# One PSUM ring for products and transposes, and W loaded over 128 partitions, in a pairwise bilinear kernel

## The chip, the cores and the metric

The kernel runs on one core of a Trainium2 chip. The metric is the device time of one execution in microseconds (us). Before the change it was 1623.27 us, the median of three runs (1620.51 to 1627.43).

Engines are named as the profile names them: PE is TensorE's matmul side, PEld its weight loads, DVE is VectorE, ACT is ScalarE, POOL is GpSimd, SP is SyncE, which here only issues DMAs. PEclk is the share of full speed that TensorE's clock was granted.

## What is computed

The input x has 4096 rows of F = 32 fields with D = 64 numbers each, W one 64x64 matrix for each of the 496 pairs (i, j) with i < j. All is float32. For each row b and each pair, the output is the product of field i with the pair's matrix, times field j element by element:

```python
vi = inputs[:, i_idx, :]
vj = inputs[:, j_idx, :]
vdotw = jnp.einsum('bpd,pde->bpe', vi, W)
inter = vdotw * vj
return inter.reshape(B, -1)
```

The output has 4096 x 31744 numbers, 520 MB, against 33.6 MB of x and 8.1 MB of W.

## The kernel before

**Tiles.** A tile is 128 rows of x; there are 32 of them, fully unrolled. The pairs of one field i are neighbours in the output, so for each i one product of [128, 64] with [64, (31 - i) * 64] gives a run of output columns, and its factors x_j are a run of columns of x itself. W is kept in SBUF for the whole run, in 16 tensors w0 to w15, one for each pair p of neighbouring fields (2p, 2p + 1): the even field's matrices on partitions 0 to 63, the odd one's on 64 to 127. The transposed x, xT, is laid out alike. So the matmuls of the two fields use two halves of the array's rows and run side by side.

**Products (L98 to L117).** A field pair's columns are cut into stretches of 1024. For each stretch and each of the two fields there is one PSUM tile `pm` of two banks (1024 float32). Matmuls cover one bank (512 columns) each, in the order first bank of the even field, first bank of the odd field, second bank of the even field, second bank of the odd field. TensorE takes its instructions in this order. A float32 matmul stands in the trace as two MATMULs, each with a weight load. The widths shrink with i: fields 0 to 15 have a first stretch of 1024 columns (the odd field 15 just so), and a narrower second one; fields 16 to 30 have a single stretch of 960 down to 64 columns. That makes 46 products a tile.

**Multiplication (L121).** VectorE multiplies each `pm` with its run of x and writes into an output buffer `o` in SBUF. This frees the `pm` slot.

**Stores (L124).** The outputs of a tile leave in ten stores, as the list STORES groups the field pairs: pairs 0 to 7 each by themselves, 8 and 9 together, 10 to 15 together. There are five output buffers. The stores are issued on SP, in order, behind the loads of W (L80), which stand on the same queue. Before each issue SP waits for what the DMA needs, and, from the ninth DMA of the program on, for an earlier DMA that used the same one of eight completion counters.

**Transposes (L63 to L70).** TensorE also transposes x: 16 blocks of 128x128 a tile, into PSUM tiles `pt` of one bank (four blocks each), which ScalarE copies to xT. The next tile's x is transposed ahead of store group 5 (PREFETCH_AT). The framework's scheduler places the four groups of one tile's transposes among the products of earlier ones.

**PSUM.** PSUM has eight banks. Three slots of two banks are for `pm`, two slots of one bank for `pt`:

```python
ps_t = ctx.enter_context(tc.tile_pool(name="ps_t", bufs=2, space=bass.MemoryType.PSUM))
ps_m = ctx.enter_context(tc.tile_pool(name="ps_m", bufs=3, space=bass.MemoryType.PSUM))
```

Slots are given out in turn: the first matmul into a slot waits until its last reader has ended.

**Loads.** x tiles come on ScalarE's queue, three buffers, two tiles ahead. W comes on SP as 31 loads over 64 partitions each (field 31 has no pairs).

Of the kernel before, what the change touches and what calls it, by code (L numbers as in the profile page):

```python
# [1 line left out]

# [6 lines left out]

F32 = mybir.dt.float32  # L10
ALU = mybir.AluOpType

P = 128  # batch rows per tile
NPS = 1024  # columns per PSUM tile (two banks)
BANK = 512  # columns per matmul
# Field pairs (i = 2p, 2p + 1) whose outputs leave in one store.
STORES = [[0], [1], [2], [3], [4], [5], [6], [7], [8, 9], [10, 11, 12, 13, 14, 15]]
PREFETCH_AT = 5  # store group before which the next tile's x is transposed


@with_exitstack
def pair_bilinear_kernel(
    ctx: ExitStack,
    tc: tile.TileContext,
    x: bass.AP,  # [B, F * D]
    w: bass.AP,  # [D, NP * D]: w[d, p * D + e] = W[p, d, e]
    out: bass.AP,  # [B, NP * D]
    F: int,
    D: int,
):  # L30
    """out[b, p, e] = x[b, j, e] * sum_d x[b, i, d] W[p, d, e] for each pair p = (i, j), i < j.

    The pairs of one i are neighbours in p, with j = i+1 .. F-1. So for each i one
    product [128, D] x [D, (F-1-i) * D] gives a run of output columns, and its
    factors x_j are the run of columns (i+1) * D .. F * D of x itself.
    Even i live on partitions 0-63 and odd i on 64-127, for W and for the
    transposed x, so that the matmuls of two i share the array's rows.
    """
    nc = tc.nc
    B = x.shape[0]  # L40
    NT = B // P
    NPR = F // 2

    width = [(F - 1 - i) * D for i in range(F)]
    off = [sum(width[:i]) for i in range(F)]
    store_w = [sum(width[2 * p] + width[2 * p + 1] for p in g) for g in STORES]

    const = ctx.enter_context(tc.tile_pool(name="const", bufs=1))
    xpool = ctx.enter_context(tc.tile_pool(name="x", bufs=3))
    xtpool = ctx.enter_context(tc.tile_pool(name="xT", bufs=2))  # L50
    opool = ctx.enter_context(tc.tile_pool(name="o", bufs=5))
    ps_t = ctx.enter_context(tc.tile_pool(name="ps_t", bufs=2, space=bass.MemoryType.PSUM))
    ps_m = ctx.enter_context(tc.tile_pool(name="ps_m", bufs=3, space=bass.MemoryType.PSUM))

    ident = const.tile([P, P], F32, tag="ident", name="ident")
    make_identity(nc, ident)

    def load_x(t):
        xt = xpool.tile([P, F * D], F32, tag="x", name=f"x_{t}")
        nc.scalar.dma_start(out=xt, in_=x[ts(t, P), :])  # L60
        return xt

    def transpose_x(t, xt):  # L63
        xT = xtpool.tile([P, NPR, P], F32, tag="xT", name=f"xT_{t}")
        for g in range(NPR // 4):
            pt = ps_t.tile([P, 4, P], F32, tag="pt", name=f"pt_{t}_{g}")
            for c in range(4):
                nc.tensor.transpose(pt[:, c, :], xt[:, ts(4 * g + c, P)], ident)  # L68
            nc.scalar.copy(xT[:, 4 * g : 4 * g + 4, :], pt)  # L69
        return xT  # L70

    xs = {0: load_x(0)}

    w_sb = []
    for p in range(NPR):
        wp = const.tile([P, width[2 * p]], F32, tag=f"w{p}", name=f"w{p}")
        for h in range(2):
            i = 2 * p + h
            if width[i]:
                nc.sync.dma_start(  # L80
                    out=wp[h * D : (h + 1) * D, : width[i]],
                    in_=w[:, off[i] : off[i] + width[i]],
                )
        w_sb.append(wp)

    xs[1] = load_x(1)
    xTs = {0: transpose_x(0, xs[0])}

    for t in range(NT):
        xt, xT = xs.pop(t), xTs.pop(t)  # L90
        if t + 2 < NT:
            xs[t + 2] = load_x(t + 2)
        for s, group in enumerate(STORES):
            if s == PREFETCH_AT and t + 1 < NT:
                xTs[t + 1] = transpose_x(t + 1, xs[t + 1])
            o0 = off[2 * group[0]]
            osb = opool.tile([P, max(store_w)], F32, tag="o", name=f"o_{t}_{s}")
            for p in group:  # L98
                for c0 in range(0, width[2 * p], NPS):
                    live = []  # L100
                    for h in range(2):
                        i = 2 * p + h
                        n = min(NPS, width[i] - c0)
                        if n > 0:
                            pm = ps_m.tile([P, NPS], F32, tag="pm", name=f"pm_{t}_{i}_{c0}")
                            live.append((h, i, n, pm))
                    for b0 in range(0, NPS, BANK):
                        for h, i, n, pm in live:
                            b1 = min(b0 + BANK, n)
                            if b1 > b0:  # L110
                                nc.tensor.matmul(  # L111
                                    pm[:, b0:b1],
                                    xT[h * D : (h + 1) * D, p, :],
                                    w_sb[p][h * D : (h + 1) * D, c0 + b0 : c0 + b1],
                                    start=True,
                                    stop=True,
                                )  # L117
                    for h, i, n, pm in live:
                        o = off[i] - o0 + c0
                        xj = (i + 1) * D + c0  # L120
                        nc.vector.tensor_tensor(  # L121
                            osb[:, o : o + n], pm[:, :n], xt[:, xj : xj + n], ALU.mult
                        )
            nc.sync.dma_start(  # L124
                out=out[ts(t, P), o0 : o0 + store_w[s]], in_=osb[:, : store_w[s]]
            )


# [18 lines left out]
```

## Time and profile before

| what | us |
|---|---|
| median of three runs | 1623.27 |
| the three runs | 1623.27, 1620.51, 1627.43 |
| span of the profiled execution | 1624.4 |
| PE busy (union) | 1400.6 (86%) |
| DVE busy | 1205.8 (74%) |
| ACT busy | 70.2 (4%) |
| mean DMA share, 104.6 to 1600 us | 0.84, 349 GB/s |

The profiled execution has no time of its own beside its span. The span lies within the runs shown, 1.1 us above their median. PE's busy time is a union of pipelined matmuls and does not mean that the array is full for 86% of the span. The mean granted clock over the run was 0.963.

The chain that ended last, followed back from the last instruction, spends 60% of the span in the products' matmuls (L111), 31% in VectorE's multiplications (L121), 4% in transposes (L68) and 3% in the loads of W. The rows on which the prediction rests are shown there.

### The profile page before, as it was taken

How to read it: one execution, taken by the hardware profiler on the slowest of the kernel's cores; microseconds unless marked ns; L12 is line 12 of the kernel's file. 1: busy time of each engine (PE TensorE's matmuls, PEld its weight loads, DVE VectorE, ACT ScalarE, POOL GpSimd, SP SyncE). 2: the span in 40 equal slices, each digit the busy share in tenths (PEclk: the TensorE clock that was granted, in tenths of full speed). 3: DMA queues.
4: the chain of work that ended last, by engine and by line, in shares of the span. 5: the costliest groups of instructions: out<-in, count | busy, mean ns of one | idle time of the engine just before them, and what ended most of it. 6: DMA issues, size and time to landing. Idle time of an engine off the chain costs nothing.

```text
span 1624.4 us, 13543 instructions
## 1 busy us (share of the span) xinstructions
PE 1400.6 (86%) x5376; PEld 680.8 (42%) x5376; DVE 1205.8 (74%) x1472; ACT 70.2 (4%) x129; POOL 0.7 (0%) x6
## 2 busy tenths in 40 slices
PE   7688888889888888888888888888888898888886
PEld 3344444444444444444444443444444444434443
DVE  4477777777867778777787777787777777777875
ACT  1000000000000000000000000000000000000000
POOL 0000000000000000000000000000000000000000
PEclk9899999999989999999999999999999989999998
DMA  9998888788877888788888878987888878888876
GB/s 243 382 383 370 357 345 348 330 371 355 348 317 321 377 361 346 319 344 347 367 362 342 346 329 376 379 362 320 343 347 373 372 318 334 342 374 367 349 298 289
DMA packets 53231, 562.66 MB, mean 346 GB/s; under 512 B 6192, under 2 KB 6576, under 8 KB 8112
## 3 DMA queue, kind: packets, MB, share of 16 engines
q1 hardware_dynamic: 48560, 528.24, 78.8%
q10 hardware_dynamic: 4608, 33.56, 5.3%
q8 instruction: 42, 0.69, 0.2%
q14 instruction: 21, 0.17, 0.0%
HBM read 41.68 MB, written 520.09 MB: 346 GB/s over the span
## 4 chain that ended last, share of the span: by engine, by line
PE 63%; DVE 31%; DMA 3%; issue 2%; SPq 0%; DVEq 0%
PE pm L111 60%; DVE o L121 31%; PE pt L68 4%; DMA w<-in_w_dram 3%; DMA out_dram<-o 0%; SPq L80 0%; DVEq L121 0%; SPq L124 0%
## 5 line engine op out<-in xcount | busy, mean ns | idle before, releaser
L111 PE MATMUL pm<-w,xT 64*128 64x512 f32 (+7 forms) x4864 | 1333.1, 567 | 210.2 <-DVE o L121 193.3
L121 DVE TENSOR_TENSOR o<-pm,x 128x1024 f32<-128x1024 f32 (+15 forms) x1472 | 1205.8, 870 | 411.3 <-PE pm L111 385.2
L111 PEld LDWEIGHTS pm<-w,xT 64*128 64x128 f32 x4864 | 623.8, 192 | 893.7 <-DVE o L121 637.3
L69 ACT COPY xT<-pt 128x512 f32<-128x512 f32 x128 | 68.9, 589 | 1467.1 <-PE pm L111 759.2
L68 PE MATMUL pt<-ident,x 128*128 128x128 f32 x512 | 78.1, 287 | 6.0 <-DMA x<-in_x_dram 6.0
L68 PEld LDWEIGHTS pt<-ident,x 128*128 128x128 f32 x512 | 56.9, 143 | 42.2 <-issue 41.3
L69 ACT ACT_TABLE_LOAD x1 | 1.3, 1283 | 2.1 <-issue 2.1
masks.py:199 POOL TENSOR_SCALAR_AFFINE_SELECT ident<-ident 128x128 f32<-128x128 f32 x1 | 0.3, 293 | 0.1
masks.py:197 POOL MEMSET ident<- 128x128 f32 x1 | 0.2, 206 | 0.3 <-POOLq L139 0.3
L139 POOL MEMSET const-bfloat16-1.0<- 128x1 bf16 x1 | 0.1, 102 | 0.0
L139 POOL MEMSET const-uint8-127<- 128x1 uint8 x1 | 0.1, 102 | 0.0
L139 POOL MEMSET const-float32-0.0<- 128x1 f32 x1 | 0.1, 99 | 0.2 <-issue 0.2
L139 POOL MEMSET const-float32-1.0<- 128x1 f32 x1 | 0.1, 98 | 0.0
## 6 DMA issues: line engine op xcount, KB each, us to landing
out_dram<-o SPq DMA_DIRECT2D x32, 2112.0 KB, 9.4
out_dram<-o SPq DMA_DIRECT2D x32, 1952.0 KB, 7.9
out_dram<-o SPq DMA_DIRECT2D x32, 1824.0 KB, 7.8
out_dram<-o SPq DMA_DIRECT2D x32, 1728.0 KB, 5.5
out_dram<-o SPq DMA_DIRECT2D x32, 1696.0 KB, 7.5
out_dram<-o SPq DMA_DIRECT2D x32, 1568.0 KB, 7.8
out_dram<-o SPq DMA_DIRECT2D x32, 1440.0 KB, 7.3
out_dram<-o SPq DMA_DIRECT2D x32, 1312.0 KB, 5.7
```

Of the source, the lines that this page charges most:

```text
L68: nc.tensor.transpose(pt[:, c, :], xt[:, ts(4 * g + c, P)], ident)
L69: nc.scalar.copy(xT[:, 4 * g : 4 * g + 4, :], pt)
L111: nc.tensor.matmul(pm[:, b0:b1], xT[h * D : (h + 1) * D, p, :], w_sb[p][h * D : (h + 1) * D, c0 + b0 : c0 + b1], start=True, stop=True,)
L121: nc.vector.tensor_tensor(osb[:, o : o + n], pm[:, :n], xt[:, xj : xj + n], ALU.mult)
L139: nc = bacc.Bacc("TRN2", target_bir_lowering=False, num_devices=1)
```

## The change

All eight banks form one pool of four slots of two banks. Products and transposes take their slots from it in the order in which they stand in the program. A transpose tile is now two banks wide: eight blocks and one ScalarE copy of 1024 columns, twice a tile instead of four times with half the width. The first half of the next tile's x is transposed ahead of store group 5, the second ahead of group 6, each in its own place.

W is laid out by the host as [128, 16384]: for each field pair the even field's matrices on the first 64 rows, the odd field's on the last 64, padded by 64 columns of zeros where the odd field has one matrix less. So each w tensor is one load over all 128 partitions, 16 in place of 31.

```diff
-    ps_t = ctx.enter_context(tc.tile_pool(name="ps_t", bufs=2, space=bass.MemoryType.PSUM))
-    ps_m = ctx.enter_context(tc.tile_pool(name="ps_m", bufs=3, space=bass.MemoryType.PSUM))
+    psum = ctx.enter_context(tc.tile_pool(name="ps", bufs=4, space=bass.MemoryType.PSUM))
...
-    def transpose_x(t, xt):
-        xT = xtpool.tile([P, NPR, P], F32, tag="xT", name=f"xT_{t}")
-        for g in range(NPR // 4):
-            pt = ps_t.tile([P, 4, P], F32, tag="pt", name=f"pt_{t}_{g}")
-            for c in range(4):
-                nc.tensor.transpose(pt[:, c, :], xt[:, ts(4 * g + c, P)], ident)
-            nc.scalar.copy(xT[:, 4 * g : 4 * g + 4, :], pt)
-        return xT
+    def transpose_x(xT, t, xt, g):
+        n = NPS // P
+        pt = psum.tile([P, NPS], F32, tag="ps", name=f"pt_{t}_{g}")
+        for c in range(n):
+            nc.tensor.transpose(pt[:, ts(c, P)], xt[:, ts(n * g + c, P)], ident)
+        nc.scalar.copy(xT[:, ts(g, NPS)], pt)
+
+    def new_xT(t):
+        return xtpool.tile([P, NPR * P], F32, tag="xT", name=f"xT_{t}")
...
-        for h in range(2):
-            i = 2 * p + h
-            if width[i]:
-                nc.sync.dma_start(
-                    out=wp[h * D : (h + 1) * D, : width[i]],
-                    in_=w[:, off[i] : off[i] + width[i]],
-                )
+        nc.sync.dma_start(out=wp, in_=w[:, woff[p] : woff[p] + width[2 * p]])
...
-            if s == PREFETCH_AT and t + 1 < NT:
-                xTs[t + 1] = transpose_x(t + 1, xs[t + 1])
+            if t + 1 < NT and s in (PREFETCH_AT, PREFETCH_AT + 1):
+                if s == PREFETCH_AT:
+                    xTs[t + 1] = new_xT(t + 1)
+                transpose_x(xTs[t + 1], t + 1, xs[t + 1], s - PREFETCH_AT)
...
-                            pm = ps_m.tile([P, NPS], F32, tag="pm", name=f"pm_{t}_{i}_{c0}")
+                            pm = psum.tile([P, NPS], F32, tag="ps", name=f"pm_{t}_{i}_{c0}")
```

On TensorE, around the transposes in the second tile. A name `pm_i_c` is the product of field i from column c on, `pt_g` a group of transposes, the last number of each name a running one; "waits" names the engine or DMA counter whose progress is waited for. Before, from the end of field pair 4 to pair 5's second stretch and the next transposes:

```order
L111 MATMUL pm_9_1024_452<-w_92,xT_243 128x384 [waits DVE_49]
L68 MATMUL pt_2_471<-ident,x_154 128x128 [waits Activation_49]
L68 MATMUL pt_2_471<-ident,x_154 128x128 x3
L68 MATMUL pt_3_477<-ident,x_154 128x128 [waits Activation_49]
L68 MATMUL pt_3_477<-ident,x_154 128x128 x3
L111 MATMUL pm_10_0_484<-w_95,xT_243 128x512 [waits DVE_49]
L111 MATMUL pm_11_0_485<-w_95,xT_243 128x512 [waits DVE_49]
L111 MATMUL pm_10_0_484<-w_95,xT_243 128x512
L111 MATMUL pm_11_0_485<-w_95,xT_243 128x512
L111 MATMUL pm_10_1024_492<-w_95,xT_243 128x320 [waits DVE_49]
L111 MATMUL pm_11_1024_493<-w_95,xT_243 128x256 [waits DVE_49]
L68 MATMUL pt_0_674<-ident,x_369 128x128 [waits DMAHW2_49,Activation_49]
```

The same place in the changed kernel:

```order
L115 MATMUL pm_9_1024_426<-w_85,xT_221 128x384 [waits DVE_49]
L72 MATMUL pt_0_433<-ident,x_132 128x128 [waits DVE_49]
L72 MATMUL pt_0_433<-ident,x_132 128x128 x7
L115 MATMUL pm_10_0_444<-w_87,xT_221 128x512 [waits DVE_49]
L115 MATMUL pm_11_0_445<-w_87,xT_221 128x512 [waits DVE_49]
L115 MATMUL pm_10_0_444<-w_87,xT_221 128x512
L115 MATMUL pm_11_0_445<-w_87,xT_221 128x512
L115 MATMUL pm_10_1024_452<-w_87,xT_221 128x320 [waits DVE_49]
L115 MATMUL pm_11_1024_453<-w_87,xT_221 128x256 [waits Activation_49]
L72 MATMUL pt_1_459<-ident,x_132 128x128 [waits DVE_49]
L72 MATMUL pt_1_459<-ident,x_132 128x128 x7
L115 MATMUL pm_12_0_470<-w_89,xT_221 128x512 [waits DVE_49]
```

The transposes now wait for VectorE (the slot's last reader) instead of ScalarE, and four tiles later in the ring a product, field 11's second part, waits for ScalarE's copy instead of VectorE.

On SP, from the last loads of W to the first stores. Before:

```order
L80 DMA w_122<-in_w_dram 64x192 [waits DMAHW7_49]
L80 DMA w_122<-in_w_dram 64x128 [waits DMAHW0_49]
L80 DMA w_125<-in_w_dram 64x64 [waits DMAHW1_49]
L124 DMA out_dram<-o_0_156 128x3904 [waits DMAHW2_49,DVE_49]
L124 DMA out_dram<-o_1_174 128x3648 [waits DMAHW3_49,DVE_49]
```

After:

```order
L83 DMA w_103<-in_w_dram 128x320 [waits DMAHW0_49]
L83 DMA w_105<-in_w_dram 128x192 [waits DMAHW1_49]
L83 DMA w_107<-in_w_dram 128x64 [waits DMAHW2_49]
L128 DMA out_dram<-o_0_134 128x3904 [waits DMAHW3_49,DVE_49]
L128 DMA out_dram<-o_1_152 128x3648 [waits DMAHW4_49,DVE_49]
```

The order on the queue is the same, with 16 loads instead of 31 ahead of the first store, each over 128 partitions and still each waiting for the DMA eight places earlier.

More of the change, by code (lines that the diff above doesn't have):

```diff
@@ L45, in pair_bilinear_kernel @@
     off = [sum(width[:i]) for i in range(F)]
+    woff = [sum(width[0 : 2 * p : 2]) for p in range(NPR)]
     store_w = [sum(width[2 * p] + width[2 * p + 1] for p in g) for g in STORES]
@@ L76, in pair_bilinear_kernel @@
         wp = const.tile([P, width[2 * p]], F32, tag=f"w{p}", name=f"w{p}")
-        for h in range(2):
-            i = 2 * p + h
-            if width[i]:
-                nc.sync.dma_start(
-                    out=wp[h * D : (h + 1) * D, : width[i]],
-                    in_=w[:, off[i] : off[i] + width[i]],
-                )
+        nc.sync.dma_start(out=wp, in_=w[:, woff[p] : woff[p] + width[2 * p]])
         w_sb.append(wp)
     xs[1] = load_x(1)
-    xTs = {0: transpose_x(0, xs[0])}
+    xTs = {0: new_xT(0)}
+    for g in range(2):
+        transpose_x(xTs[0], 0, xs[0], g)
     for t in range(NT):
@@ L112, in pair_bilinear_kernel @@
                                     pm[:, b0:b1],
-                                    xT[h * D : (h + 1) * D, p, :],
+                                    xT[h * D : (h + 1) * D, ts(p, P)],
                                     w_sb[p][h * D : (h + 1) * D, c0 + b0 : c0 + b1],
@@ L136 @@
     x = np.ascontiguousarray(r_inputs).reshape(B, F * D)
-    w = np.ascontiguousarray(np.transpose(L0_rec_W, (1, 0, 2))).reshape(D, NP * D)
+    wt = np.transpose(L0_rec_W, (1, 0, 2))
+    n = [F - 1 - i for i in range(F)]
+    first = [sum(n[:i]) for i in range(F)]
+    halves = [
+        np.concatenate(
+            [
+                np.pad(wt[:, first[i] : first[i] + n[i]], ((0, 0), (0, h), (0, 0)))
+                for i in range(h, F, 2)
+            ],
+            axis=1,
+        )
+        for h in range(2)
+    ]
+    w = np.ascontiguousarray(np.stack(halves)).reshape(2 * D, -1)
     nc = bacc.Bacc("TRN2", target_bir_lowering=False, num_devices=1)
```

## The prediction

> **What bounds the kernel now.** I read the waits first, then VectorE's timeline over one tile, then the chain, then the DMA share by stretches. The waits (who waited for whom: us in total, times, longest):
>
> ```profile
> DVE o L121 <- PE pm L111: 385.2, 384, 16.3
> PE pm L111 <- DVE o L121: 193.3, 347, 10.1
> DVE o L121 <- DMA out_dram<-o: 13.7, 1, 13.7
> SPq L80 <- DMA w<-in_w_dram: 25.0, 20, 3.9
> ```
>
> TensorE and VectorE wait for each other, VectorE for a store once. The stretches (us; busy time of PE, PEld, DVE, ACT, POOL; PEclk, DMA share, GB/s), the second being one whole tile:
>
> ```profile
> 10.20:47.20 37.00, 30.50 (x112) 13.30 (x112) 19.79 (x20) 2.73 (x5) 0.00 (x0) 1.00 0.99 237
> 178.93:227.32 48.39, 42.12 (x170) 20.28 (x168) 37.69 (x47) 2.15 (x4) 0.00 (x0) 1.00 0.86 358
> 57.00:107.00 50.00, 43.73 (x167) 21.82 (x163) 37.24 (x45) 2.15 (x4) 0.00 (x0) 0.95 1.00 419
> 980.00:1000.00 20.00, 17.41 (x70) 7.60 (x68) 16.41 (x18) 1.07 (x2) 0.00 (x0) 1.00 1.02 432
> ```
>
> At full clock a tile takes 48.39 us. VectorE works 37.69 of them, and the DMA share of 0.86 leaves room. Nobody is full: two engines pass three PSUM slots to and fro. VectorE's timeline of that tile (start, length, count, then the idle time before):
>
> ```profile
> 178.93 4.61 DVE L121 TENSOR_TENSOR o<-pm,x 128x1024 f32<-128x1024 f32 x4 [1.61 <-PE pm L111]
> 183.78 4.34 DVE L121 TENSOR_TENSOR o<-pm,x 128x1024 f32<-128x1024 f32 x4 [0.23 <-PE pm L111]
> 188.49 4.08 DVE L121 TENSOR_TENSOR o<-pm,x 128x1024 f32<-128x1024 f32 x4 [0.37 <-PE pm L111]
> 193.06 3.79 DVE L121 TENSOR_TENSOR o<-pm,x 128x1024 f32<-128x1024 f32 x4 [0.50 <-PE pm L111]
> 197.49 3.35 DVE L121 TENSOR_TENSOR o<-pm,x 128x1024 f32<-128x1024 f32 x4 [0.63 <-PE pm L111]
> 202.65 3.08 DVE L121 TENSOR_TENSOR o<-pm,x 128x1024 f32<-128x1024 f32 x4 [1.81 <-PE pm L111]
> 207.49 2.82 DVE L121 TENSOR_TENSOR o<-pm,x 128x1024 f32<-128x1024 f32 x4 [1.75 <-PE pm L111]
> 211.91 2.49 DVE L121 TENSOR_TENSOR o<-pm,x 128x1024 f32<-128x1024 f32 x3 [1.61 <-PE pm L111]
> 215.10 2.15 DVE L121 TENSOR_TENSOR o<-pm,x 128x960 f32<-128x960 f32 x2 [0.70 <-PE pm L111]
> ...
> 227.32 2.35 DVE L121 TENSOR_TENSOR o<-pm,x 128x1024 f32<-128x1024 f32 x2 [1.61 <-PE pm L111]
> ```
>
> These nine waits make 9.21 us of the 10.70 idle. The chain tells what each consists of (start, us, what):
>
> ```profile
> 187.31 1.15 PE pm L111 x4
> ...
> 199.68 1.02 PE pt L68 x8
> 200.70 1.97 PE pm L111 x8
> ```
>
> A pair's first tile is ready 1.15 us after the slot of its **second** tile comes free, because TensorE's order puts that tile's first bank ahead of the first tile's second bank. It is ready 1.97 us after its **own** slot comes free. Check on before, with three slots: when the partner's slot comes free ahead of 193.06, the operation of 640 columns is left, about 0.7 us. 1.15 - 0.7 is 0.45, and that row's own wait is 0.50. At the start of a tile two narrow operations, about 0.35 us, remain: 1.97 - 0.35 = 1.62, measured 1.61.
>
> **The ring, part by part.** Matmuls, products, transposes (512) and bytes stored stay as they are. With four slots VectorE has one operation more to do while TensorE refills, so I go through a tile by the same rule. An operation pair of two times 1024 takes 2.35 (last timeline row), so of each four the rest is the narrow pair.
>
> Field pairs 0 to 4: the own slot comes free three operations ahead. The three shortest, ahead of pair 4, are 1024, 576 and 512, together about 1.14 + 1.3 = 2.4 > 1.97; the partner's slot leaves two, at least 1.3 > 1.15. So 0.23, 0.37, 0.50 and 0.63 go to nothing, and so do the like waits among pairs 8 to 11.
>
> Pair 5: the transposes take the slot that the first 1024 operation of pair 4 frees. Their 1.02 us lie beside the second one (about 1.14). Then come 1.97, and VectorE has 3.35 - 2.35 = 1.00 left: wait **1.0**. Pair 6 likewise: 1.97 - (3.08 - 2.35 = 0.73) = **1.25**. Pair 7: 1.97 - 1.14 - (2.82 - 2.35 = 0.47) = **0.35**. Next tile: now 1.61, less one more narrow operation, 192 columns:
>
> ```profile
> L121 DVE TENSOR_TENSOR o<-pm,x 128x192 f32<-128x192 f32 x64 | 22.5, 352 | 0.0
> L69 ACT COPY xT<-pt 128x512 f32<-128x512 f32 x128 | 68.9, 589 | 1467.1 <-PE pm L111 759.2 <-PE pt L68 708.0
> ```
>
> That operation is worth about 0.27 beside its neighbours: **1.35**. Sum 3.95. A tile takes 37.69 + 3.95 = 41.6 us. Back-to-back operations overlap by some 0.08 (2.35 against 2 x 1.22), so eight waits fewer may take off another 0.6; a slot freed late puts on as much. I take **41.5**.
>
> New on TensorE: the matmul that reuses a transpose's slot (fields 11 and 13, second part) waits for ScalarE's copy, and all products behind it queue there. A 128x1024 copy isn't in the trace; it lies between 0.59 (one of 512, row above) and 1.18 (two), and I take the upper end. Nothing shows: transposes and copy end 1.02 + 1.18 = 2.2 us after the slot came free, and TensorE arrives 1.14 + 1.97 = 3.1 us after it. A copy 1 us longer than this cover would cost 1 us twice a tile, 64 us in all.
>
> **W and the start.** Sixteen loads bring 16,384 columns x 128 x 4 = 8.39 MB in place of 8.13. They ran at 237 GB/s (10.2 to 47.2, share 0.99) over 64 partitions; transfers over 128 run at 419. With three x tiles that is 11.5 MB / 419 = 27.5 us, so all is there at about 29 us. The stores stand behind the loads on SP:
>
> ```profile
> 0.74 46.33 SPq L80 DMA_DIRECT2D w<-in_w_dram  x31
> 47.20 4.54 SPq L124 DMA_DIRECT2D out_dram<-o  x5
> ...
> 16.29 1.22 DVE L121 TENSOR_TENSOR o<-pm,x 128x1024 f32<-128x1024 f32 x1 [16.29 <-PE pm L111]
> 53.59 1.23 DVE L121 TENSOR_TENSOR o<-pm,x 128x1024 f32<-128x1024 f32 x1 [13.67 <-DMA out_dram<-o]
> ```
>
> The first store leaves at about 27 us, not 47.20, so the 13.67 us stall on the sixth output buffer shrinks to about 2 (VectorE wants it at 12.3 + 20.2; the store needs 27 + 5). First VectorE work: x and W's first load (2.1 MB at 419, some 7 us with the first bytes), transposes 1.0, copy 1.2, products 2.0, transposes of the second half 1.0: **12.3** instead of 16.29.
>
> **The clock.** Most tiles are slower than 48.39. In the first row here VectorE does 1380 operations, 30 tiles of 46, from the second tile's start to the last one's: 1487.13 / 30 = 49.57 us a tile. The next two show why:
>
> ```profile
> 80.63:1567.76 1487.13, 1302.47 (x5034) 632.18 (x5032) 1130.48 (x1380) 63.36 (x118) 0.00 (x0) 0.97 0.84 350
> 451.30:458.40 7.10, 5.73 (x27) 3.59 (x29) 4.61 (x7) 0.00 (x0) 0.00 (x0) 1.00 0.80 331
> 458.40:465.20 6.80, 6.01 (x16) 3.71 (x14) 2.82 (x4) 0.00 (x0) 0.00 (x0) 0.50 0.72 299
> 1613.25 3.85 DVE L121 TENSOR_TENSOR o<-pm,x 128x512 f32<-128x512 f32 x9 [0.48 <-PE pm L111]
> ```
>
> After the sparse stretch around the transposes the granted clock falls to 0.50. That costs 1.2 us a tile, 37 us in all. The waits there shrink by a good half (1.81 + 1.75 + 1.61 to 1.0 + 1.25 + 0.35), so I keep a third, **12**; the ends are 0 and 37.
>
> The Trainium skill, "TensorE: Matmul & The Clock Gate", section "HAM oscillation — how this bites in real kernels", asks for gaps over about 3.4 us before the clock drops. By it this term would be nothing and the sum 1350. The trace disagrees: TensorE was busy 5.73 of the 7.10 us ahead of the drop.
>
> **Sum, on the profiled execution** (span 1624.4, beside a median of 1623.27; no correction): 12.3 + 32 x 41.5 + 2 + 12 + 7.3 = **1362**. The 7.3 is the end now: VectorE's last row ends at 1613.25 + 3.85 = 1617.1, then the last store.
>
> **Rivals.**
>
> *DMA becomes the bound.* A tile moves (562.66 MB of the page less W) / 32 = 17.3 MB:
>
> ```profile
> DMA packets 53231, 562.66 MB, mean 346 GB/s; under 512 B 6192, under 2 KB 6576, under 8 KB 8112
> HBM read 41.68 MB, written 520.09 MB: 346 GB/s over the span
> ```
>
> It decides below 17.3 / 41.5 = 417 GB/s. At 419 to 432 the transfers alone need 562.9 / 419 = 1343 to 1303 us, beneath the forecast. But those rows last 50 us at most; a sustained 400 gives 1407 + 8 = 1415. Chance 0.14.
>
> *DMA is bound already.* The tile above runs at 358 GB/s. The Trainium skill, "DMA: Bandwidth & Descriptors", section "Where 436 GB/s comes from", has the HBM side bind at about 358 per core. If that rate held over a whole run, 562.9 / 358 + 8 = 1580. The rows of 419 and 432, and VectorE's single wait for a store, speak against it; chance 0.04.
>
> *The clock keeps its toll:* 37 in place of 12, 1387. The waits at pairs 5 and 6 stay sparse. Chance 0.14.
>
> *Only W helps:* the ring gives nothing if the waits aren't for slots, and 4.0 + 11.7 us at the start remain: 1609. Against it stands 1.15 us of TensorE after each VectorE release. Chance 0.06.
>
> *Slower:* copies and products lock each other. If ScalarE's copy takes twice the estimate, each of two places a tile grows from 1.8 to 1.02 + 1.18 + 1.97 = 4.2 us. If at the same time the fourth slot is always held and helps nowhere, 2 x 2.4 x 32 = 154 comes on top of 1609: 1763. It decides from 2 x (copy beyond its cover) over 6.9 us a tile, what the ring saves. Chance 0.03.
>
> **How the numbers follow.** The forecast has 0.59. Its own ends: clock 0 and tiles at 41.0 give 1334; an early start, which the DMA floor of 1303 to 1343 limits, a little less; the clock's other end 1387. With most of the sustained-DMA case the range is 1325 to 1410. A measurement of this kernel tells about 0.5% (8 us) from no change. All cases but the last lie beyond that on the fast side; for a near-tie I leave 0.02.
>
> **What would show it.** Right: no wait of 0.23 to 0.63 in VectorE's rows of pairs 0 to 4; about 1.0, 1.25, 0.35 and 1.35 at pairs 5, 6, 7 and the next tile; first store near 27 us; PEclk 0.50 rarer; DMA share near 1. Wrong: VectorE's waits for stores in the hundreds of us (DMA bound), long rows of TensorE waiting for ScalarE (copy uncovered), or the clock low as often as before.

## The result and the profile after

The changed kernel takes 1350.3 us, the median of four runs (1349.9 to 1350.42), against 1623.5 us before (four runs, 1620.51 to 1627.43). The ratio is 0.8325, with a 95% interval of 0.8286 to 0.8365. The forecast was 1362 us, in a range of 1325 to 1410.

The profiled execution spans 1348.6 us and took 1350.42. First the waits of the changed kernel (us in total, times, longest). L115, L125 and L128 are the old L111, L121 and L124:

```profile
DVE o L125 <- PE pm L115: 152.0, 125, 15.2
PE pm L115 <- DVE o L125: 35.2, 72, 1.7
DVE o L125 <- DMA out_dram<-o: 18.0, 22, 2.3
```

VectorE's waits for products fell from 385.2 to 152.0 us, in 125 waits instead of 384: four a tile. Its timeline over one tile shows which four:

```profile
59.62 19.11 DVE L125 TENSOR_TENSOR o<-pm,x 128x1024 f32<-128x1024 f32 x20 [1.48 <-PE pm L115]
79.81 3.08 DVE L125 TENSOR_TENSOR o<-pm,x 128x1024 f32<-128x1024 f32 x4 [1.08 <-PE pm L115]
84.24 2.82 DVE L125 TENSOR_TENSOR o<-pm,x 128x1024 f32<-128x1024 f32 x4 [1.34 <-PE pm L115]
87.53 11.51 DVE L125 TENSOR_TENSOR o<-pm,x 128x1024 f32<-128x1024 f32 x18 [0.48 <-PE pm L115]
100.53 19.11 DVE L125 TENSOR_TENSOR o<-pm,x 128x1024 f32<-128x1024 f32 x20 [1.48 <-PE pm L115]
```

Field pairs 0 to 4, twenty operations in five rows before, are one unbroken row now. The waits left are those ahead of pairs 5, 6, 7 and the next tile: 1.08, 1.34, 0.48 and 1.48 us. The prediction had 1.0, 1.25, 0.35 and 1.35.

The stretches of the changed kernel (us; PE, PEld, DVE, ACT, POOL busy; PEclk, DMA share, GB/s) are that tile, and then thirty tiles (VectorE's 1380 operations are 30 times 46):

```profile
59.62:100.53 40.91, 39.61 (x170) 20.79 (x168) 36.53 (x47) 2.02 (x2) 0.00 (x0) 1.00 1.01 427
59.62:1301.73 1242.11, 1197.97 (x5042) 624.79 (x5040) 1096.36 (x1380) 60.73 (x60) 0.00 (x0) 1.00 1.00 419
```

A tile goes at 40.91 us where nothing disturbs it, and at 1242.11 / 30 = 41.40 on average. The DMA share is 1.00 over the whole 1.24 ms, where it was 0.84, and the clock was all but full. Which of the two, engines or DMA, sets the 41.40 can't be read from these rows alone: the DMA is full, and PE is busy 96% of the time. The experiments had to say.

The start and the end, on SP's and VectorE's timelines:

```profile
27.16 113.16 SPq L128 DMA_DIRECT2D out_dram<-o  x30
```

```profile
15.21 19.11 DVE L125 TENSOR_TENSOR o<-pm,x 128x1024 f32<-128x1024 f32 x20 [15.21 <-PE pm L115]
35.97 3.09 DVE L125 TENSOR_TENSOR o<-pm,x 128x1024 f32<-128x1024 f32 x4 [1.65 <-PE pm L115]
41.36 2.82 DVE L125 TENSOR_TENSOR o<-pm,x 128x1024 f32<-128x1024 f32 x4 [2.30 <-DMA out_dram<-o]
45.36 2.49 DVE L125 TENSOR_TENSOR o<-pm,x 128x1024 f32<-128x1024 f32 x3 [1.18 <-DMA out_dram<-o]
49.08 9.06 DVE L125 TENSOR_TENSOR o<-pm,x 128x960 f32<-128x960 f32 x15 [1.24 <-DMA out_dram<-o]
...
1327.96 11.51 DVE L125 TENSOR_TENSOR o<-pm,x 128x1024 f32<-128x1024 f32 x18 [0.48 <-PE pm L115]
```

The first store leaves at 27.16 us, and the single stall of 13.67 us has become three of 2.30, 1.18 and 1.24.

### The profile page after: what moved, and what is told of

The parts are those of the page before. It is cut to its first block, busy times and chain, and to the rows that moved or that the text cites. A ratio compares the mean times of both kernels' runs of the same rounds, so it can differ in the third digit from the quotient of the medians.

```text
span 1348.6 us, 13450 instructions
## 1 busy us (share of the span) xinstructions
PE 1281.7 (95%) x5376; PEld 666.9 (49%) x5376; DVE 1169.4 (87%) x1472; ACT 66.1 (5%) x65; POOL 0.7 (0%) x6
## 4 chain that ended last, share of the span: by engine, by line
PE 70%; DVE 16%; DMA 10%; issue 3%; DVEq 0%
PE pm L115 66%; DVE o L125 16%; DMA out_dram<-o 10%; PE pt L72 4%; DMA x<-in_x_dram 1%; DVEq L125 0%; DVEq L162 0%
## 5 line engine op out<-in xcount | busy, mean ns | idle before, releaser
L125 DVE TENSOR_TENSOR o<-pm,x 128x1024 f32<-128x1024 f32 (+15 forms) x1472 | 1169.4, 866 | 170.0 <-PE pm L115 152.0
L115 PE MATMUL pm<-w,xT 64*128 64x512 f32 (+6 forms) x4864 | 1214.4, 539 | 37.2 <-DVE o L125 35.2
L115 PEld LDWEIGHTS pm<-w,xT 64*128 64x128 f32 x4864 | 610.5, 186 | 622.7 <-DVE o L125 404.3
L73 ACT COPY xT<-pt 128x1024 f32<-128x1024 f32 x64 | 64.8, 1012 | 1216.2 <-PE pt L72 1180.0
L72 PE MATMUL pt<-ident,x 128*128 128x128 f32 x512 | 71.4, 284 | 20.1 <-DVE o L125 11.6
```

The source lines that it names most:

```text
L72: nc.tensor.transpose(pt[:, ts(c, P)], xt[:, ts(n * g + c, P)], ident)
L73: nc.scalar.copy(xT[:, ts(g, NPS)], pt)
L115: nc.tensor.matmul(pm[:, b0:b1], xT[h * D : (h + 1) * D, ts(p, P)], w_sb[p][h * D : (h + 1) * D, c0 + b0 : c0 + b1], start=True, stop=True,)
L125: nc.vector.tensor_tensor(osb[:, o : o + n], pm[:, :n], xt[:, xj : xj + n], ALU.mult)
```

## The experiments

Times are one run each unless a count is given; the kernel before, run beside them, lay between 1617 and 1650 us. So small differences among these kernels are read against the changed kernel and in the traces. Line numbers shift with each edit: the multiplication of VectorE is L125 in the changed kernel, L131 with the ring alone, L116 with W alone and L121 without transposes.

**Which part brought what.** The ring with W laid out on the host and loaded as before (only the loads are shown):

```diff
-        nc.sync.dma_start(out=wp, in_=w[:, woff[p] : woff[p] + width[2 * p]])
+        for h in range(2):
+            i = 2 * p + h
+            if width[i]:
+                nc.sync.dma_start(
+                    out=wp[h * D : (h + 1) * D, : width[i]],
+                    in_=w[:, off[i] : off[i] + width[i]],
+                )
...
```

> The ring of four slots with W loaded as before (31 loads over 64 partitions). If the ring carries the gain in the steady tiles and W's layout only the start: first store near 47 us again, VectorE stalls some 14 us on the sixth output buffer, the second tile begins near 80 us instead of 59.6, every later tile stays at about 41.4, total about 1368 us. If W's layout matters in the steady tiles too (it feeds every matmul): tiles near 48, total near 1600 us.

Measured: 1367.71 us. VectorE's timeline of this kernel has the old stall again, and the second tile's start at 77.14 instead of 59.62:

```profile
54.35 3.08 DVE L131 TENSOR_TENSOR o<-pm,x 128x1024 f32<-128x1024 f32 x4 [15.56 <-DMA out_dram<-o]
...
77.14 3.42 DVE L131 TENSOR_TENSOR o<-pm,x 128x1024 f32<-128x1024 f32 x3 [1.48 <-PE pm L121]
```

The 17.5 us lost at the start are the whole difference from 1350.3. W's layout does nothing for the steady tiles. At the start the DMA share is near 1 in both kernels, but it moves 237 GB/s in the kernel before (10.2 to 47.2 us) and 419 in the changed one (3 to 26 us). So the transfers themselves got faster; whether by their 128 partitions or by their smaller number, no run tells apart.

The other half, W alone, with pools and transposes of before. This is the edit against the kernel before (the host's layout of W, not shown, is that of the change):

```diff
-        for h in range(2):
-            i = 2 * p + h
-            if width[i]:
-                nc.sync.dma_start(
-                    out=wp[h * D : (h + 1) * D, : width[i]],
-                    in_=w[:, off[i] : off[i] + width[i]],
-                )
+        nc.sync.dma_start(out=wp, in_=w[:, woff[p] : woff[p] + width[2 * p]])
...
```

> The three product slots and two transpose slots of before, with W in 16 loads over 128 partitions. By the same theory: tiles at 48.4 at full clock and 49.6 on average as before, first store near 27 us, total about 1608 us (4 us earlier first product, 11 us less stall). By the rival that W's layout carries the gain: about 1400 us or less.

Measured: 1623.52 us, beside 1642.62 for the kernel before. The first store leaves at 27.28 us and the second tile starts at 67.75 instead of 80.64. The old waits are all there:

```profile
72.60 4.35 DVE L116 TENSOR_TENSOR o<-pm,x 128x1024 f32<-128x1024 f32 x4 [0.23 <-PE pm L106]
77.31 4.08 DVE L116 TENSOR_TENSOR o<-pm,x 128x1024 f32<-128x1024 f32 x4 [0.37 <-PE pm L106]
81.89 3.80 DVE L116 TENSOR_TENSOR o<-pm,x 128x1024 f32<-128x1024 f32 x4 [0.50 <-PE pm L106]
86.32 3.35 DVE L116 TENSOR_TENSOR o<-pm,x 128x1024 f32<-128x1024 f32 x4 [0.63 <-PE pm L106]
91.48 3.08 DVE L116 TENSOR_TENSOR o<-pm,x 128x1024 f32<-128x1024 f32 x4 [1.81 <-PE pm L106]
```

The place is as expected; the total missed 1608 by 15 us. Its thirty tiles from 67.75 to 1568.77 take 50.03 us on average where the kernel before took 49.57, 14 us in all, at a mean clock of 0.957 against 0.963. The scatter of this slot arrangement is as large as the gain sought, so the total alone would not have shown it.

**Is it the fourth slot?**

```diff
-    psum = ctx.enter_context(tc.tile_pool(name="ps", bufs=4, space=bass.MemoryType.PSUM))
+    psum = ctx.enter_context(tc.tile_pool(name="ps", bufs=3, space=bass.MemoryType.PSUM))
```

> The changed kernel with three slots of two banks in the shared ring and two banks unused. Slot theory (a pair is ready 1.97 us after its own slot and 1.15 us after its partner's came free): the waits of 0.23, 0.37, 0.50, 0.63 come back in field pairs 1 to 4, and the transposes now take one of three slots, so their two waits grow beyond the 1.8 of before; tiles of about 49 us at full clock, total 1590 to 1640 us. If not the number of slots but the order of the transposes, or one copy instead of two, brought the gain: tiles near 41, total about 1350 us.

Measured: 1694.43 us, slower than the kernel before. VectorE's timeline, four rows of one tile and one of a later tile:

```profile
184.89 3.80 DVE L125 TENSOR_TENSOR o<-pm,x 128x1024 f32<-128x1024 f32 x4 [0.50 <-PE pm L115]
189.32 3.35 DVE L125 TENSOR_TENSOR o<-pm,x 128x1024 f32<-128x1024 f32 x4 [0.63 <-PE pm L115]
194.78 3.08 DVE L125 TENSOR_TENSOR o<-pm,x 128x1024 f32<-128x1024 f32 x4 [2.10 <-PE pm L115]
200.23 2.82 DVE L125 TENSOR_TENSOR o<-pm,x 128x1024 f32<-128x1024 f32 x4 [2.37 <-PE pm L115]
...
464.12 2.82 DVE L125 TENSOR_TENSOR o<-pm,x 128x1024 f32<-128x1024 f32 x4 [4.01 <-PE pm L115]
```

The clock around the transposes of the first of these tiles, in the form of the stretches:

```profile
196.00:203.00 7.00, 4.87 (x24) 2.87 (x25) 4.63 (x8) 1.01 (x1) 0.00 (x0) 1.00 0.79 333
204.00:210.00 6.00, 5.21 (x14) 3.27 (x12) 2.49 (x3) 0.00 (x0) 0.00 (x0) 0.50 0.65 272
```

The small waits return to the hundredth (0.50, 0.63), so they are the missing slot's. At the transposes, with the clock still full, the waits are 2.10 and 2.37 instead of 1.81 and 1.75: with three slots the shared ring does harm. In the later tile the clock falls sooner, to 0.50 from 460 to 462 us, and the second wait grows to 4.01. The tiles take 52.45 us on average instead of the 49 expected, at a mean clock of 0.931 over the run, and so the total missed 1590 to 1640. The two waits alone are 0.9 us a tile more than before at full clock; how the rest divides between further waits and the clock was not taken apart.

This kernel has the same wide transposes with one copy each, in the same places, and only one slot less. So these alone bring no gain: it takes the fourth slot.

**Does the ScalarE copy have cover?**

```diff
-        nc.scalar.copy(xT[:, ts(g, NPS)], pt)
+        for _ in range(2):
+            nc.scalar.copy(xT[:, ts(g, NPS)], pt)
```

> The changed kernel with each ScalarE copy of transposes done twice, 1.01 us longer, both before the slot is given on. Cover theory: transposes and two copies end 1.0 + 2.05 = 3.1 us after the slot came free, about when TensorE arrives there (1.14 + 1.97); loss 0 to 0.3 us twice a tile, total 1350 to 1365 us. If ScalarE's copy stands on the path already: 1.0 us twice a tile, about 1415 us.

Measured: 1349.03 us. VectorE's waits in an undisturbed tile are 1.08, 1.34, 0.48 and 1.48 again. The total says little here, because the DMA sets it, as the next runs show; the waits say that a second copy of 1.01 us never reaches VectorE in the steady tiles. It is at the very edge of the cover that was worked out: TensorE's weight loads now wait for ScalarE 30 times from 60 to 1300 us, up to 0.2 us each. At the start the second copy isn't hidden: the first multiplication comes at 16.89 us instead of 15.21.

**Engines or DMA?** Three kernels take load off the one or the other, one adds an output buffer and two add bytes. First the transposes left out:

```diff
-        xt, xT = xs.pop(t), xTs.pop(t)
+        xt, xT = xs.pop(t), xTs[0]
...
-            if t + 1 < NT and s in (PREFETCH_AT, PREFETCH_AT + 1):
...
-                transpose_x(xTs[t + 1], t + 1, xs[t + 1], s - PREFETCH_AT)
```

> The changed kernel without any transpose after the first tile's: all tiles multiply with the first tile's transposed x, so the products are left wrong in 31 tiles and TensorE and ScalarE save their part. If TensorE and VectorE bound the changed kernel by themselves: the waits at field pairs 5 and 6 (1.08 and 1.34 us) go, tiles of about 39.0, total about 1275 us. If the DMA is a floor just beneath: it takes over at 421 to 427 GB/s, 17.3 MB a tile or 40.6 to 41.1 us, VectorE's waits for stores grow from 18 us to over 40, total 1325 to 1340 us.

Measured: 1348.78 us, as long as with all transposes. What the engines save comes back as waiting for stores:

```profile
DVE o L121 <- DMA out_dram<-o: 83.8, 72, 3.8
DVE o L121 <- PE pm L111: 83.1, 88, 14.1
```

Where no store is waited for, a tile of this kernel takes 39.24 us (1260.20 to 1299.44), near the 39.0 expected of the engines alone. On average its thirty tiles still take 41.34. So there is a floor, and it lies 9 us above the range expected: the sustained rate here is 419 GB/s (100 to 1300 us), not 421 to 427. Then half of each store left out:

```diff
-                out=out[ts(t, P), o0 : o0 + store_w[s]], in_=osb[:, : store_w[s]]
+                out=out[ts(t, P), o0 : o0 + store_w[s] // 2],
+                in_=osb[:, : store_w[s] // 2],
```

> The changed kernel with every store cut to the first half of its columns (half of the output isn't written), all else the same. It takes the DMA out of the way. If the engines set the pace and the DMA adds only the waits of the start and of some tiles: every tile at 40.9 us, no wait of VectorE for a store, total 15.2 + 32 x 40.9 + some 5 = 1329 us, 20 us under the changed kernel. If the DMA's traffic also slows the engines themselves (SBUF reads beside VectorE's writes): VectorE's 1024-column operation falls below 1.21 us and tiles below 40.5.

Measured: 1324.78 us. Thirty tiles of this kernel:

```profile
55.36:1282.60 1227.24, 1188.15 (x5042) 623.36 (x5040) 1096.07 (x1380) 60.74 (x60) 0.00 (x0) 1.00 0.56 224
```

That is 40.91 us a tile at 224 GB/s, and VectorE's busy time is the same to 0.03% (1096.07 against 1096.36). The engines set 40.91, and DMA traffic of 419 GB/s beside them doesn't slow them against 224. Rate and landing time remain to be told apart, by 15 sixteenths of each store, and by a sixth output buffer:

```diff
-                out=out[ts(t, P), o0 : o0 + store_w[s]], in_=osb[:, : store_w[s]]
+                out=out[ts(t, P), o0 : o0 + store_w[s] // 16 * 15],
+                in_=osb[:, : store_w[s] // 16 * 15],
```

> The changed kernel with each store cut to the first 15 sixteenths of its columns (the rest of the output isn't written). A tile then moves 16.3 MB. If the DMA's rate (419 GB/s) is what holds the changed kernel at 41.4 us a tile: 38.9 us are needed, less than the engines' 40.9, so tiles at 40.9, next to no wait for stores after the start, total 1325 to 1332 us. If it is the time a store takes to land (14 us) with five output buffers, which 6% fewer bytes hardly change: total 1342 us or more.

```diff
-    opool = ctx.enter_context(tc.tile_pool(name="o", bufs=5))
+    opool = ctx.enter_context(tc.tile_pool(name="o", bufs=6))
```

> The changed kernel with six output buffers instead of five. If the rate holds it: VectorE waits less for stores at the start, but the same bytes take the same time: 1345 to 1351 us. If landing time and buffers hold it: tiles at 40.9 and about 1330 us.

Measured: 1332.97 us with fewer bytes, 1348.96 us with six buffers (four runs, 1348.72 to 1349.14; ratio to before 0.8268, interval 0.8204 to 0.8332). The stretch of thirty tiles with fewer bytes:

```profile
59.30:1286.00 1226.70, 1187.61 (x5038) 622.81 (x5036) 1096.03 (x1380) 60.72 (x60) 0.00 (x0) 1.00 0.97 399
```

6% fewer bytes bring the tiles to 1226.70 / 30 = 40.89 on average (the total is 1 us above the range expected). The sixth buffer removes the stall of the start (its second tile begins at 55.98) and changes the end by 1.3 us: the stores then queue longer (a typical store takes 18 us from issue to landing instead of 14) and the bytes take the same time. So it is the rate. More bytes must then cost in proportion. The first try stored a sixteenth of each store a second time, in a small store of its own:

```diff
+            nc.sync.dma_start(
+                out=out[ts(t, P), o0 : o0 + store_w[s] // 16],
+                in_=osb[:, : store_w[s] // 16],
+            )
             nc.sync.dma_start(
                 out=out[ts(t, P), o0 : o0 + store_w[s]], in_=osb[:, : store_w[s]]
```

> The changed kernel with the first sixteenth of each store's columns stored a second time, in a store of its own ahead of the full one; the output is the same. A tile moves 18.3 MB. If the DMA's rate holds the kernel: 18.3 MB / 419 = 43.8 us a tile, total 1420 to 1435 us, and VectorE waits for stores 80 us or more. If engines and DMA only graze each other: about 1360 us.

Measured: 1592.59 us, far above both. SP's own waits show where the kernel stood (L132 is the full store):

```profile
SPq L132 <- DMA out_dram<-o: 513.4, 112, 11.0
```

The full stores stood on SP waiting for other stores, the DMA share fell to 0.92 over the steady tiles, and the rate to 374 GB/s. So this run says little about the rate of a full DMA. Why it is so slow stays open: it has twice as many stores, and the added ones have rows of 0.5 to 1 KB. The test was repeated with about the same bytes in one large store a tile:

```diff
-            nc.sync.dma_start(
-                out=out[ts(t, P), o0 : o0 + store_w[s]], in_=osb[:, : store_w[s]]
-            )
+            for _ in range(1 + (s == 7)):
+                nc.sync.dma_start(
+                    out=out[ts(t, P), o0 : o0 + store_w[s]], in_=osb[:, : store_w[s]]
+                )
```

> The changed kernel with the store of field pair 7 (1.08 MB, rows of 8.4 KB) issued twice in each tile; the output is the same. About as many bytes more as with the sixteenths stored twice, but in one large store, one DMA more a tile. If the rate of 419 GB/s holds the kernel: 18.4 MB a tile or 43.9 us, total 597.5 MB / 419 + 8 = about 1434 us, DMA share 1.00. If the sixteenths cost what they did because of the number of bytes: about 1590 us. If engines and DMA only graze each other: 1350 to 1365 us.

Measured: 1442.09 us. Thirty tiles of this kernel, and VectorE's wait for stores:

```profile
59.66:1380.90 1321.24, 1221.11 (x5043) 631.37 (x5041) 1098.28 (x1381) 60.76 (x60) 0.00 (x0) 0.99 0.99 417
```

```profile
DVE o L125 <- DMA out_dram<-o: 128.5, 107, 3.2
```

44.04 us a tile at 417 GB/s, as the rate says (43.9 at 419); the total is 8 us above the 1434 expected. 6.1% more bytes make the kernel 6.8% longer. SP waits for other stores here too, 402.0 us in all, and the DMA stays full. So such waits are not by themselves what slowed the sixteenths.

**Can the transposes go elsewhere?** Ahead of store groups 1 and 2, with full stores, and then with half of each as above:

```diff
-PREFETCH_AT = 5
+PREFETCH_AT = 1
```

> The changed kernel with the transposes ahead of store groups 1 and 2 instead of 5 and 6. Slot theory: there two wide operations (about 1.81 to 2.08 us) cover the 1.97 us, so the waits of 1.08 and 1.34 shrink to 0.2 or less, and pairs 5 to 7 keep 0 to 0.5; tiles of about 39.5 us by the engines alone. With the DMA floor of 40.6 to 41.1 us a tile: total 1330 to 1342 us, about 1% under the changed kernel, and more waiting for stores. Without such a floor: about 1300 us. If the waits at pairs 5 and 6 come from the transposes as such and not from the narrow operations around them: no change, 1350 us.

> The transposes ahead of store groups 1 and 2, with every store cut to its first half (half of the output isn't written), so that the engines show alone what the earlier place does. From the undisturbed tiles of the run with full stores: 40.6 us a tile in place of 40.9, total about 1315 us. By the rule of 1.97 us alone (39.5 us a tile): about 1280 us.

Measured: 1348.9 us with full stores (four runs, 1348.01 to 1352.18; the changed kernel has 1350.3), and 1313.76 us with half stores, against 1324.78 at the old place. VectorE's timeline with half stores:

```profile
95.31 4.42 DVE L125 TENSOR_TENSOR o<-pm,x 128x1024 f32<-128x1024 f32 x4 [1.48 <-PE pm L115]
100.02 4.15 DVE L125 TENSOR_TENSOR o<-pm,x 128x1024 f32<-128x1024 f32 x4 [0.28 <-PE pm L115]
105.03 10.73 DVE L125 TENSOR_TENSOR o<-pm,x 128x1024 f32<-128x1024 f32 x12 [0.86 <-PE pm L115]
116.00 3.08 DVE L125 TENSOR_TENSOR o<-pm,x 128x1024 f32<-128x1024 f32 x4 [0.24 <-PE pm L115]
119.58 2.82 DVE L125 TENSOR_TENSOR o<-pm,x 128x1024 f32<-128x1024 f32 x4 [0.50 <-PE pm L115]
```

The waits at pairs 5 and 6 shrink to 0.24 and 0.50, but 0.28 and 0.86 appear ahead of pairs 1 and 2, where the slot rule allowed 0.2 or less. The tile gains only 0.34 us (40.57) and not the 1.4 that the rule gave (39.5). The chain that ended last, for the stretch from 95 to 108 us of this kernel, tells why:

```profile
94.85 2.20 PE pm L115 x11
97.05 1.02 PE pt L72 x8
98.07 3.99 PE pm L115 x15
102.06 1.02 PE pt L72 x8
103.08 4.35 PE pm L115 x17
```

TensorE works without a break there and waits for no slot. A rule that counts from a slot's release can't see this wait: beside the widest field pairs TensorE has no idle time into which the transposes could go. With full stores the total misses the 1330 to 1342 expected. Taken alone it would fit the third case, no change, but the waits did move. In the full kernel none of the gain arrives, because the DMA sets the end.

## Why the prediction was right, and where it was not

| term | predicted | measured in the profile |
|---|---|---|
| first VectorE operation | 12.3 | 15.21 |
| first tile beyond the steady ones | 2 | 44.41 - 40.91 = 3.5 |
| tiles by the engines alone | 41.5 | 40.91 |
| the clock | 12 in all | about 1.5 (one drop) |
| waiting for stores in tiles 1 to 30 | 0 | 18.0 - 4.7 = 13.3 |
| last tile | 41.5 | 37.7 |
| end after VectorE's last operation | 7.3 | 9.1 |

**The slot rule held for the change.** The four waits sum to 4.38 us where 3.95 were worked out, each about 0.1 us over: the rule leaves out the time from a release to the next start (ahead of pair 6 the chain has 0.04, 0.04 and 0.02 us of it). The waits of pairs 0 to 4 went, and three slots bring them back. The 128x1024 copy, taken at 1.18 us, lasts 1.01. The rule failed once, with the transposes at pairs 1 and 2, where TensorE itself was the limit. That VectorE's busy time per tile fell from 37.69 to 36.53, because back-to-back operations overlap, was allowed for with 0.6 us and came to 1.16. So the engines' tile was mis-sized by 0.6 us, 18 us over 31 tiles.

**W and the start.** The kernel with the ring alone put the worth of W's layout at 17.4 us, in the first 77 us and nowhere else. The first store's time was right (27.16 for 27). The first operation comes 2.9 us later than said. Half of it is x, which arrived at 8.5 us where some 7 were allowed. Another 1.1 us is the first products, which start at 12.12 and take 3.1 us instead of 2.0: pairs of weight loads come 0.85 us apart at 13.14 and 13.99, and 0.43 apart from 14.59 on. Why stays open; the granted clock reads 1.00 there.

**The clock.** This term was to keep a third of its 37 us and kept almost nothing: one drop of about 3.4 us in the steady tiles (near 1177 us). The means are 0.996 with four slots, 0.963 before and 0.931 with the three shared slots, in the order of VectorE's waits for products (152, 385 and 466 us). That the sparse stretches cause the drops fits all three; it was not tried by itself. The order by VectorE's waits doesn't hold everywhere: the kernel with the sixteenths stored twice has 179 us of them and a clock of 0.939. The share of time in which PE is busy fits better, though it is no proof: over thirty tiles it is 96% with four slots, 88% before, 87% with three slots and 86% with the sixteenths, at clocks of 1.00, 0.97, 0.93 and 0.94. The Trainium skill's rule of gaps over 3.4 us ("TensorE: Matmul & The Clock Gate", section "HAM oscillation — how this bites in real kernels") gave 1350 for the sum, and lands on the measured time, but not by its mechanism: with three slots the mean clock fell to 0.931, with stretches at 0.50, though TensorE's longest wait for a slot was 1.1 us.

**What binds: the step that failed.** The prediction had the way and the size of the gain right, but took the engines as the bound after the change, and gave "DMA becomes the bound" 0.14, at a sustained 400 GB/s. The DMA is the bound, at the 419 that the 50 us row had shown. That rival's own line, 562.9 MB / 419 + 8, gives 1351 us, and the kernel takes 1350.3. Two things hid it. The engines' tile came out 0.6 us shorter than said, which moves the deciding rate from 417 to 17.3 / 40.91 = 423 GB/s, above the 419. And the range of rates from 419 to 432 was read as a floor safely beneath the forecast, when its lower end, with the 8 us of start and end, was within 11 us of it. Its sign of a DMA bound, waits for stores in the hundreds of us, would have missed this one: with the two bounds 0.5 us a tile apart, VectorE waits 18.0 us in all. That the total came within 12 us is in part luck, since errors cancelled: the engines' term was 18 us too long, and the last tile and the clock another 14, while the waits for stores, the start and the end were about 20 too short. The engines alone would give 1325 us (half stores).

**The other rivals.** The rate of 358 GB/s fell: 419 held for 1.24 ms. Only W helping fell with the ring-only run. The slower case has a real mechanism, transposes and products sharing too few slots (1694 us with three). The copy was not its cause: there TensorE's weight loads waited 11.5 us in all for ScalarE. Four slots cover even a doubled copy in the steady tiles.

## What to carry to other kernels

Follow each buffer: how much work the reader still has when the writer's slot comes free, against the time the writer needs from there. The difference is the wait, and one slot more changes it by one operation's length; this gave the four waits left in the changed kernel's tile within about 0.13 us. It holds only while the writer waits for slots; with the transposes moved to pairs 1 and 2 the writer had no idle time left, and the rule was 0.7 us short. And when a change takes an engine's slack away, compare the new pace with the bytes per tile over the rate that full stretches sustain, at the low end of those rows: here the next bound (1350 us) lay 2% above what the engines alone would give (1325 us), and neither of the two savings tried on the engines reached the end.

## What the runs showed of the hardware that was not expected

A second small store ahead of each full one, 6% more bytes, cost 18% (1592.59 us), and one large store more, 6.1%, cost 6.8%. The bytes are about the same, so the number of stores, their short rows or the order in which they wait on the queue weighed more than the bytes; which of them was not tried. The granted clock fell to 0.50 (204 to 210 us with three slots) in a kernel in which TensorE never waited longer than 1.1 us for a slot.
